# Two graph-attention layers over 64 graphs: a round laid out anew by engine, the caps on ScalarE, another column order for the left sides, and another start

## The chip, the cores and the metric

The kernel runs on one core of a Trainium2 chip. The time is the device time of one launch in microseconds, the median of three runs. A core has five engines with a queue each: TensorE (PE) multiplies matrices, VectorE (DVE), ScalarE (ACT) and GpSimd (POOL) work on elements, and SyncE (SP) here only issues transfers. Each engine takes its queue strictly in order, and engines wait for each other through semaphores.

## The reference

There are 64 graphs of N = 256 nodes with D = 512 features, and an adjacency matrix `adj` of zeros and ones for each. Two residual layers follow each other:

```python
h = jnp.maximum(_layernorm(x, axis=-1), 0.0)
x = x + _L0_gnn_ref(adj, h, ...)     # two GAT layers
h = jnp.maximum(_layernorm(x, axis=-1), 0.0)
x = x + _L1_gnn_ref(h, adj, ...)     # one attention layer, 8 heads of 64
```

The first GAT layer has 4 heads of 256 features (512 -> 1024, then elu), the second one head (1024 -> 512). For each head `e = leaky_relu(asrc[s] + adst[d])`, where `asrc` and `adst` are products of the projected features with the attention vectors. It is masked by `adj` with the diagonal set, and a softmax over the sources s is applied to the projected features. The last layer does the same with 8 heads, but its mask is `adj` alone, its softmax runs over the other axis, and a row without neighbours gets equal weights. Everything is float32.

## The kernel before

`short_path` does the work; `general_path` is entered only when an exponential leaves a safe range, which these inputs don't cause.

Graphs are handled one at a time on 128 partitions, as T = 2 tiles of 128 nodes. A graph goes through four products and three attentions:

- `m1a` and `m1b`: the normalised input times the two halves of W1 (heads 0 and 1, heads 2 and 3), then `gat1`;
- `m2`: the elu output times W2, then `gat2`;
- `m3`: the normalised sum times W_proj, then `gat3`.

**A product** (class `Product`) is a 2x2 block product with seven block multiplications in place of eight. The left side `a` holds seven blocks: four are turned parts of h, the other three and one replaced block are sums, made by `left` on GpSimd (L208 to L215). The right side `w` holds seven as well, made once by `right` on DVE (L489). The seven multiplications are the steps p1 to p7. p1, p6, p7 and p4 add into one PSUM tile `sum`; between them ACT copies the sum out (`kept`, L60: s1, u2, u3). p2, p5 and p3 go to tiles `pm`. `put` adds a copy and a `pm` on DVE (L246), or copies the sum on ACT (L244), into `xl`. In the code's order p3 may start only when c22 has read the same `pm`, p7 only when u2 is copied, and p6 and p5 only when GpSimd has made s2 and s1.

The columns that give `asrc` and `adst` ride along as extra columns of W (four in m1a, one in m2, eight in m3). They are computed at the start as dot products on DVE (`dot`, L494; for W_proj on GpSimd and DVE, L555 and L557).

**An attention** takes the logits, makes three exponentials on ACT (L268, L430) and sends one of them through DRAM to all partitions (`spread`, L233 and L238: a transfer out, and one or more transfers back into `bc`). exp(leaky_relu(a+o)) is then a maximum of two products: for each head and source tile ACT scales the row (`wy`, L273), and DVE takes the maximum and applies the mask (L274). That makes `e`. TensorE multiplies `e` by `xl` (`gat1` L348, `gat2` L399, `gat3` L447), where a column of ones gives the sum of the softmax. `gat3` works with tiles 64 columns wide, the others with 128. DVE divides (`out1` L356 and L358, `out2` L405 and L408, `out3` L453 and L455), and for `out3` GpSimd adds the result to x2 (L457). `elu1` follows on ACT and DVE (L361, L362, L367).

**masks** (L289 to L299) makes, from the integer matrix, `mask` with the diagonal and `a01` without it, counts each row (`deg`), and scales `a01` to the caps of layer three: a huge number where there is an edge, and a tiny one in every column of a row without neighbours. `cap3` turns the caps with transposing DMAs.

**The turns.** h of layer one (`norm1`, L186) is turned by a trip through DRAM (`away`, L200 and L201) that changes the order of blocks, and a 32x32 block transpose on DVE (`back`, L206). The z tiles of `turn2` and h of `turn3` are turned by TensorE (L193) and copied by ACT (L376, L226).

**What sets the order.** The kernel schedules by hand: each engine's queue is the order in which the Python code issues. `order` is a list of items, such as `-2 edges3 0`, and is gone through once for each round r; the number is added to r to give the graph. A round therefore mixes layer three of graph r-2, layer two of r-1 and the first of r. The pieces of the weight work (`weights_for_0`, `weights_for_1`) are issued one after each item in rounds 0 and 1, the rest ahead of turn2 and turn3.

**Buffers.** PSUM has 2 `sum`, 4 `pm` and 2 `pt` tiles. `e` has eight buffers, `wy` three, and the copies s1, u2 and u3 have two each.

**The start** loads graph 0 and W1 in 32 transfers, in an order of rows that fits the block order of `away`. It makes the 32 dots for W1's extra columns, turns graph 0 by way of DRAM and begins with m1a.

Of the kernel before, what the change touches and what calls it, by code (L numbers as in the profile page):

```python
# [17 lines left out]
P = 128  # L18
# [19 lines left out]
class Product:  # L38
# [19 lines left out]
    def kept(self, name):  # L58
        s = self.work.tile([P, 268], F32, name=name)
        self.nc.scalar.activation(s[:, :self.n], self.sum[:, :self.n], AF.Copy)  # L60
        return s

    def p1(self):
        self.sum = self.ps_sum.tile([P, 512], F32, name="sum")
        self.product(self.sum, 0, True, False)
        self.s1 = self.kept("s1")
# [10 lines left out]
    def p6(self):  # L77
        self.product(self.sum, 2, False, False)
        self.u2 = self.kept("u2")

    def p7(self):
        self.product(self.sum, 4, False, False)
        self.u3 = self.kept("u3")
# [14 lines left out]
def short_path(ctx, tc, flags, x, adj, w1, att_src1, att_dst1, b1, w2, att_src2, att_dst2, b2, w_proj, w_att,  # L98
# [84 lines left out]
    def norm(src, rstd, off):  # L183
        h = work.tile([P, T, D], F32, name="h", bufs=1)
        for t in range(T):
            nc.scalar.activation(h[:, t, :], src[:, t, :], AF.Relu, bias=off[:, t:t + 1],  # L186
                                 scale=rstd[:, t:t + 1])
        return h
# [6 lines left out]
    def away(h):  # L195

        kept = dram.tile([T, 4, P, P], F32, name="kept_h")
        nc.sync.dma_start(kept.rearrange("t a p e -> p t a e"), h.rearrange("p t (a e) -> p t a e", a=4))  # L200
        nc.sync.dma_start(h, kept.rearrange("t a (j q) e -> (a j) t (q e)", q=4))  # L201
# [74 lines left out]
    class Graph:  # L276


        def __init__(self, b):
            self.b = b  # L280

# [6 lines left out]
        def masks(self):  # L288

            self.mask = work.tile([P, T, N], BF16, name="mask")  # L290
            nc.vector.scalar_tensor_tensor(self.mask, self.ad, 0.0, eye, ALU.is_gt, ALU.max)
            a01 = self.a01 = work.tile([P, T, N], BF16, name="a01", bufs=1)
            nc.vector.tensor_scalar(a01, self.ad, 0.0, None, ALU.is_gt)
            deg = small.tile([P, T], F32, name="deg")
            nc.vector.tensor_reduce(deg, a01, AX.X, ALU.add)
            none = small.tile([P, T], F32, name="none")
            nc.vector.tensor_scalar(none, deg, 0.5, EVEN, ALU.is_lt, ALU.mult)
            for t in range(T):
                nc.vector.tensor_scalar(a01[:, t, :], a01[:, t, :], OPEN, none[:, t:t + 1], ALU.mult, ALU.add)  # L299
# [12 lines left out]
        def norm1(self):  # L312
            self.h = norm(self.xs, *self.ro)
# [7 lines left out]
        def turn1(self):  # L321
            a = left_of(self.h, True)
            self.m1 = [Product(nc, ps_sum, ps_mm, work, a, w1_sb[i], put1(i)) for i in range(2)]
            self.e = {}
# [12 lines left out]
        def edges1(self, h):  # L337
            e = self.e[1, h] = work.tile([P, T, N], F32, name="e", bufs=8)
            for s in range(T):
                weigh(e[:, s, :], self.bc1[h], self.ex1[:, h, s:s + 1], self.ex1[:, H1 + h, s:s + 1],  # L340
                      self.mask[:, s, :], ALU.mult)

        def gat1(self, g, t):
            self.pms = []
            for h in (2 * g, 2 * g + 1):
                pm = ps_mm.tile([P, 512], F32, name="pm")
                for s in range(T):
                    nc.tensor.matmul(pm[:, :Q + 1], self.e[1, h][:, s, t * P:(t + 1) * P], xl1[:, s, h, L1:],  # L348
                                     start=(s == 0), stop=(s == T - 1))
                self.pms.append((h, pm))  # L350

        def out1(self, g, t):
            z = self.zt[t]
            for h, pm in self.pms:
                r = small.tile([P, 1], F32, name="r1")
                nc.vector.reciprocal(r, pm[:, Q:Q + 1])  # L356
                sl = slice(h * F1, (h + 1) * F1)
                nc.vector.scalar_tensor_tensor(z[:, sl], pm[:, :Q], r, b1_sb[:, sl], ALU.mult, ALU.add)  # L358

            ez = work.tile([P, 2 * F1], F32, name="ez")  # L360
            nc.scalar.activation(ez, z[:, 2 * g * F1:2 * (g + 1) * F1], AF.Relu, scale=-1.0)  # L361
            nc.scalar.activation(ez, ez, AF.Exp, scale=-1.0)  # L362
            self.e["ez", g, t] = ez
# [21 lines left out]
        def edges2(self):  # L385
            e = self.e[2] = work.tile([P, T, N], F32, name="e", bufs=8)
            for s in range(T):
                weigh(e[:, s, :], self.bc2[0], self.ex2[:, 0, s:s + 1], self.ex2[:, 1, s:s + 1],
                      self.mask[:, s, :], ALU.mult)

        def gat2(self, t):
            if t == 0:
                self.x2 = work.tile([P, T, D], F32, name="x2")
            self.pms = []
            for half in range(2):
# [5 lines left out]
                self.pms.append(pm)  # L401

        def out2(self, t):
            r = small.tile([P, 1], F32, name="r2")
            nc.vector.reciprocal(r, self.pms[0][:, Q:Q + 1])  # L405
            for half in range(2):
                sl = slice(half * Q, (half + 1) * Q)
                nc.vector.scalar_tensor_tensor(self.x2[:, t, sl], self.pms[half][:, :Q], r, self.xs[:, t, sl],  # L408
# [10 lines left out]
        def norm3(self):  # L419
            self.h = norm(self.x2, *self.ro)  # L420
# [13 lines left out]
        def edges3(self, h):  # L434
            e = self.e[3, h] = work.tile([P, T, N], F32, name="e", bufs=8)
# [4 lines left out]
        def gat3(self, a, t):  # L440
            pm = self.pm = ps_mm.tile([P, 512], F32, name="pm")
# [8 lines left out]
        def out3(self, a, t):  # L450
            pv = self.pm[:, :G * (K3 + 1)].rearrange("p (h k) -> p h k", h=G)
# [21 lines left out]
    def bring(w, src, at, r, by, squares=False):  # L473

        nk, n = w.shape[2], w.shape[3]
        for half in range(2):
            dst = blocks(w)[r][half][:, :, n - Q:]
            cols = src[:, at + half * Q:at + (half + 1) * Q]
            if squares:
                for a in range(4):  # L480
                    by[half].dma_start(dst[32 * a:32 * (a + 1)], cols[a * P:(a + 1) * P].rearrange(
                        "(c i) f -> i c f", c=4)[:, r * nk:(r + 1) * nk])
            else:
                by[half].dma_start(dst, cols.rearrange("(c p) f -> p c f", p=P)[:, r * nk:(r + 1) * nk])
# [12 lines left out]
    att2 = [work.tile([P, D2], F32, name="e", bufs=8) for i in range(2)]  # L497
# [3 lines left out]
    for r in range(2):  # L501
        for i in range(2):
            bring(w1_sb[i], w1, 2 * Q * i, r, (nc.sync, nc.scalar), squares=True)
        if r == 0:
            nc.scalar.dma_start(att1[1].rearrange("p h f -> p (h f)"), rows_of(att_dst1, HF))
    graphs[0].stats1()
    graphs[0].norm1()
    graphs[0].away1()
# [9 lines left out]
    for r in range(2):  # L518
        for s in range(2):
            for h in range(H1):  # L520
                for c in range(2):
                    dot(blocks(w1_sb[0])[r][s][:, c, h:h + 1], blocks(w1_sb[h // 2])[r][h % 2][:, c, -Q:], att1[s][:, h, :])
            if r == 1 and s == 0:
                graphs[0].turn1()
# [3 lines left out]
    def weights_for_0():  # L528
        yield from right(w1_sb[1])
        graphs[0].masks()  # L530
        graphs[0].bias()
# [14 lines left out]
    def weights_for_1():  # L546
# [17 lines left out]
        -1 exp2, -2 edges3 0, 0 m1a p2, 0 m1a p5, -2 edges3 1, 0 m1a p6, -2 edges3 2, 0 m1b p1,  # L564
        -2 edges3 3, 0 m1a p7, 0 m1a c22, -2 edges3 4, 0 m1b p2, 0 m1a p4, 0 m1a p3, 0 exp1, -2 edges3 5,
        -2 gat3 0 0, -2 out3 0 0, 0 m1b p6, -1 edges2, -2 edges3 6, 0 m1b p5, -2 gat3 0 1, -2 out3 0 1, -2 edges3 7,
        0 m1b p7, 0 m1b c22, -1 gat2 0, -1 out2 0, -1 stats3 0, 0 edges1 0, 0 m1b p4, 0 m1b p3,
        -1 gat2 1, 0 edges1 1, -1 out2 1, 0 edges1 2, 0 edges1 3, 1 load, 0 gat1 0 0, 0 out1 0 0, -2 gat3 1 0,
        -2 out3 1 0, 0 cap3, -1 stats3 1, 0 gat1 0 1, -1 norm3, 0 out1 0 1, -2 gat3 1 1, 0 elu1 0 0, -2 out3 1 1, -2 store,
        0 gat1 1 0, 0 out1 1 0, -1 turn3, 0 elu1 0 1, 0 gat1 1 1, 0 out1 1 1, 0 elu1 1 0, 0 elu1 1 1,  # L570
        -1 m3 p1, 1 stats1, -1 m3 p2, 0 turn2 0 0, 0 turn2 0 1, -1 m3 p5, -1 m3 p6, 0 turn2 1 0, 0 turn2 1 1,
        1 norm1, 1 away1, 0 m2 p1, -1 m3 p7, -1 m3 c22, 1 masks, 0 m2 p2, -1 m3 p4, -1 m3 p3, -1 exp3,
        -2 range, 0 m2 p6, 0 m2 p5, 1 turn1, 0 m2 p7, 0 m2 c22, 1 m1a p1, 0 m2 p4, 1 bias, 0 m2 p3
    """
    graphs[0].m1[0].p1()
    order = [item.split() for item in order.split(",")]
    later = {0: (weights_for_0(), "turn2"), 1: (weights_for_1(), "turn3")}
    for r in range(B + 2):
        pieces, by = later.get(r, (iter(()), ""))
        for off, what, *args in order:  # L580
            b = r + int(off)
            if not 0 <= b < B:
                continue
            if what == by:
                for _ in pieces:
                    pass
# [8 lines left out]
            next(pieces, None)  # L595
# [274 lines left out]
```

## Time and profile before

| | before |
|---|---|
| time, median of 3 | 3387.74 us (3386.66 to 3388.05) |
| span of the profiled execution | 3383.4 us |
| PE busy | 3230.2 us (95%) |
| DVE busy | 2503.5 us (74%) |
| ACT busy | 1868.1 us (55%) |
| POOL busy | 1245.1 us (37%) |
| the masks op L291, mean of 64 | 1620 ns |
| norm1 and norm3, L186, mean | 811 and 807 ns |

In the profile's lines the first number of a timeline row is its start, the second its length, both in us, and the brackets give idle time of the engine and what ended it. A float32 multiplication appears as two instructions. Matmuls are pipelined: the length of one row overlaps the next, so the distance between two starts is what an item really costs. A row of a stretch gives the busy time of the engines in the order PE, PEld (weight loads, which overlap PE), DVE, ACT, POOL, then the granted clock of TensorE, the share of the DMA engines and GB/s.

### The profile page before, as it was taken

How to read it: one execution, taken by the hardware profiler on the slowest of the kernel's cores; microseconds unless marked ns; L12 is line 12 of the kernel's file. 1: busy time of each engine (PE TensorE's matmuls, PEld its weight loads, DVE VectorE, ACT ScalarE, POOL GpSimd, SP SyncE). 2: the span in 40 equal slices, each digit the busy share in tenths (PEclk: the TensorE clock that was granted, in tenths of full speed). 3: DMA queues.
4: the chain of work that ended last, by engine and by line, in shares of the span. 5: the costliest groups of instructions: out<-in, count | busy, mean ns of one | idle time of the engine just before them, and what ended most of it. 6: DMA issues, size and time to landing. Idle time of an engine off the chain costs nothing. (4 is left out here: it accounts for less than half of the span.)

```text
span 3383.4 us, 60097 instructions
## 1 busy us (share of the span) xinstructions
PE 3230.2 (95%) x21764; PEld 2659.8 (79%) x21764; DVE 2503.5 (74%) x6447; ACT 1868.1 (55%) x4481; POOL 1245.1 (37%) x1369
## 2 busy tenths in 40 slices
PE   4899999999999999999999999999999999999996
PEld 3688888888878888878888888888888888888885
DVE  7577777777777777787777777777777777777774
ACT  2355555555565565565565565565555555555553
POOL 1433433433433433433433434434334334334332
PEclk8999999999999999999999999999999999999997
DMA  4223333323323323323333233232333333332331
GB/s 131 63 86 83 83 81 88 82 81 82 89 76 83 91 78 83 89 80 83 85 84 84 82 87 83 81 88 78 86 88 78 87 83 83 87 82 84 86 73 47
DMA packets 354349, 281.41 MB, mean 83 GB/s; under 512 B 159616, under 2 KB 254848, under 8 KB 354048
## 3 DMA queue, kind: packets, MB, share of 16 engines
q1 hardware_dynamic: 352480, 275.40, 30.1%
q8 instruction: 177, 2.90, 0.4%
q10 hardware_dynamic: 1568, 2.10, 0.2%
q14 instruction: 124, 1.02, 0.1%
HBM read 201.07 MB, written 67.96 MB: 80 GB/s over the span
## 5 line engine op out<-in xcount | busy, mean ns | idle before, releaser
L273 ACT ACTIVATE wy<-bc,exs 128x256 f32<-128x256 f32 x1664 | 776.5, 521 | 257.5 <-DMA bc<-kept 142.1
L457 POOL TENSOR_TENSOR x<-x,o 128x256 f32<-128x256 f32 x256 | 198.7, 776 | 1431.4 <-DVE o L455 1342.8
L274 DVE SCALAR_TENSOR_TENSOR e<-wy,exs,cap 128x256 f32<-128x256 f32 x1024 | 484.7, 511 | 140.4 <-ACT wy L273 132.8
L348 PE MATMUL pm<-xl,e 128*128 128x257 f32 x2048 | 518.8, 391 | 32.0 <-DVE r L356 24.8
L54 PE MATMUL sum<-w_sb,h1s 128*128 128x257 f32 x2048 | 493.8, 383 | 0.7 <-ACT u L60 0.7
L348 PEld LDWEIGHTS pm<-xl,e 128*128 128x128 f32 x2048 | 362.6, 190 | 118.0 <-PE pm L348 46.2
L246 DVE TENSOR_TENSOR xl<-pm,u 128x256 f32<-128x256 f32 (+2 forms) x512 | 215.3, 421 | 310.0 <-PE pm L54 249.7
L54 PEld LDWEIGHTS sum<-w_sb,h1s 128*128 128x128 f32 x2048 | 379.9, 190 | 73.7 <-issue 21.9
L54 PE MATMUL pm<-w_sb,h1s 128*128 128x257 f32 x1536 | 365.3, 379 | 0.0
L60 ACT ACTIVATE u<-sum 128x260 f32<-128x260 f32 (+3 forms) x512 | 195.4, 382 | 287.0 <-PE sum L54 281.4
L447 PEld LDWEIGHTS pm<-xl,e 128*64 128x64 f32 x8192 | 265.9, 139 | 99.1 <-issue 52.2
L54 PEld LDWEIGHTS pm<-w_sb,h1s 128*128 128x128 f32 x1536 | 291.2, 190 | 44.0
L212 POOL TENSOR_TENSOR hs<-hs 128x256 f32<-128x256 f32 x128 | 127.0, 992 | 518.0 <-DVE hs L206 330.6
L274 DVE SCALAR_TENSOR_TENSOR e<-wy,exs,mask 128x256 f32<-128x256 f32 x640 | 303.7, 524 | 17.2 <-ACT wy L273 9.9
L447 PE MATMUL pm<-xl,e 128*64 128x65 f32 x8192 | 302.1, 227 | 12.9 <-DVE e L274 12.6
L54 PE MATMUL sum<-w1a_sb,hs 128*128 128x260 f32 x1024 | 274.7, 391 | 36.1 <-DMA e<-in_L_gnn_att_src_dram 28.9
L54 PE MATMUL sum<-wp_sb,hs 128*128 128x264 f32 x1024 | 277.3, 393 | 9.3 <-ACT u L60 1.1
L54 PE MATMUL sum<-w1b_sb,hs 128*128 128x256 f32 x1024 | 277.4, 393 | 1.0 <-ACT u L60 1.0
L358 DVE SCALAR_TENSOR_TENSOR z<-pm,r,b_sb 128x256 f32<-128x256 f32 x512 | 247.8, 484 | 18.2
L54 PEld LDWEIGHTS sum<-w1a_sb,hs 128*128 128x128 f32 x1024 | 188.4, 190 | 89.4 <-ACT u L60 31.8
L367 DVE SCALAR_TENSOR_TENSOR z<-ez,z 128x512 f32<-128x512 f32 x256 | 206.7, 808 | 64.0 <-ACT ez L362 64.0
L399 PE MATMUL pm<-xl,e 128*128 128x257 f32 (+1 forms) x1024 | 244.1, 381 | 2.5 <-DVE e L274 2.5
(92 smaller groups left out, 5221.7 us busy)
## 6 DMA issues: line engine op xcount, KB each, us to landing
bc<-kept SPq DMA_DIRECT2D x384, 256.0 KB, 3.8
xs<-in_x_dram SPq DMA_DIRECT2D x64, 512.0 KB, 4.0
kept_h<-h SPq DMA_DIRECT2D x64, 512.0 KB, 3.2
h<-kept_h SPq DMA_DIRECT2D x64, 512.0 KB, 3.6
out_dram<-x SPq DMA_DIRECT2D x64, 512.0 KB, 2.8
ad<-in_adj_dram SPq DMA_DIRECT2D x64, 256.0 KB, 4.3
bc<-kept SPq DMA_DIRECT2D x64, 128.0 KB, 4.3
w_sb<-in_L_gnn_W_dram SPq DMA_DIRECT2D x4, 512.0 KB, 9.2
```

What stands on the lines that cost most here:

```text
L54: self.nc.tensor.matmul(to[:, :self.n], self.lhs[:, i, c, :], self.rhs[:, i, c, :], start=(first and c == 0), stop=(last and c == self.nk ...
L60: self.nc.scalar.activation(s[:, :self.n], self.sum[:, :self.n], AF.Copy)
L212: nc.gpsimd.tensor_tensor(s1, s3, a22, ALU.add)
L246: nc.vector.tensor_tensor(dst, pm, add, ALU.add)
L273: nc.scalar.activation(wy, bc, AF.Copy, scale=yw)
L274: nc.vector.scalar_tensor_tensor(dst, wy.rearrange("p t q -> p (t q)"), xw, mask, ALU.max, op)
L348: nc.tensor.matmul(pm[:, :Q + 1], self.e[1, h][:, s, t * P:(t + 1) * P], xl1[:, s, h, L1:], start=(s == 0), stop=(s == T - 1))
L358: nc.vector.scalar_tensor_tensor(z[:, sl], pm[:, :Q], r, b1_sb[:, sl], ALU.mult, ALU.add)
L367: nc.vector.scalar_tensor_tensor(z, self.e["ez", g, t], -1.0, z, ALU.add, ALU.max)
L399: nc.tensor.matmul(pm[:, :n], self.e[2][:, s, t * P:(t + 1) * P], xl2[:, s, half, L2:L2 + n], start=(s == 0), stop=(s == T - 1))
L447: nc.tensor.matmul(pv[q:q + 64, h, :], self.e[3, a * G + h][:, s, t * P + q:t * P + q + 64], xl3[:, s, a * G + h, :], start=(s == 0), stop ...
L457: nc.gpsimd.tensor_tensor(to, to, o.rearrange("p h k -> p (h k)"), ALU.add)
```

## The change

The change has five parts.

1. **The round's order.** The list `order` is replaced. In it the two tiles of `gat3` stand side by side, several `gat` and `out` items have other items between them, the copies and adds of m1a are spread over the end of one round and the start of the next, and `store` belongs to graph r-3. So that a `gat` may be issued before the `out` of an earlier one, `pms` becomes a dictionary by layer, group and tile. Rounds run from -1 to B+2, and the weight pieces are issued from round -1 on, one list after the other.
2. **The caps on ScalarE.** `masks` keeps two DVE ops: `a01` from the integers, and `mask` as the maximum of `a01` and the diagonal in bf16. Counting the rows, which is now a by-product of a copy on ACT, and the scaling go to ACT, and the small comparison to GpSimd, in a new item `caps` that stands between m2 c22 and exp2.
3. **Columns in another order.** Row 4p+c of W1 now goes to partition p, so that each partition reads contiguous rows, in one transfer where there were four. To fit, `norm1` reads x with a stride of four elements and writes h in the order that `away` needs.
4. **Buffers.** The copies s1, u2 and u3 share one name with four buffers; `e` has nine.
5. **The start.** Graph 0 is normalised by `norm0` and turned by TensorE (`turn0`) without the trip through DRAM. W1's second half is loaded first, and m1b of graph 0 goes first, with the dots for the extra columns issued between its steps; m1a follows in round -1.

```diff
-    def kept(self, name):
-        s = self.work.tile([P, 268], F32, name=name)
+    def kept(self):
+        s = self.work.tile([P, 264], F32, name="kept", bufs=4)
...
+    def mixed(h):
+        return h.rearrange("p (a c i) -> p a c i", a=4, c=4)
+
+    def unmixed(x):
+        return x.rearrange("p (a i c) -> p a c i", a=4, c=4)
...
-            nc.scalar.activation(h[:, t, :], src[:, t, :], AF.Relu, bias=off[:, t:t + 1],
-                                 scale=rstd[:, t:t + 1])
+            to, of = (mixed(h[:, t]), unmixed(src[:, t])) if mix else (h[:, t, :], src[:, t, :])
+            nc.scalar.activation(to, of, AF.Relu, bias=off[:, t:t + 1], scale=rstd[:, t:t + 1])
...
-            self.mask = work.tile([P, T, N], BF16, name="mask")
-            nc.vector.scalar_tensor_tensor(self.mask, self.ad, 0.0, eye, ALU.is_gt, ALU.max)
             a01 = self.a01 = work.tile([P, T, N], BF16, name="a01", bufs=1)
             nc.vector.tensor_scalar(a01, self.ad, 0.0, None, ALU.is_gt)
+            self.mask = work.tile([P, T, N], BF16, name="mask")
+            nc.vector.tensor_tensor(self.mask, a01, eye, ALU.max)
+
+        def caps(self):
+            a01 = self.a01
             deg = small.tile([P, T], F32, name="deg")
-            nc.vector.tensor_reduce(deg, a01, AX.X, ALU.add)
+            for t in range(T):
+                same = work.tile([P, N], BF16, name="same", bufs=1)
+                nc.scalar.activation(same, a01[:, t, :], AF.Copy, accum_out=deg[:, t:t + 1])
             none = small.tile([P, T], F32, name="none")
-            nc.vector.tensor_scalar(none, deg, 0.5, EVEN, ALU.is_lt, ALU.mult)
+            nc.gpsimd.tensor_scalar(none, deg, 0.5, EVEN, ALU.is_lt, ALU.mult)
             for t in range(T):
-                nc.vector.tensor_scalar(a01[:, t, :], a01[:, t, :], OPEN, none[:, t:t + 1], ALU.mult, ALU.add)
+                nc.scalar.activation(a01[:, t, :], a01[:, t, :], AF.Identity, bias=none[:, t:t + 1], scale=OPEN)
...
+        def turn0(self):
+            a = work.tile([P, 7, DC // 2, P], F32, name="hs")
+            for t in range(T):
+                pm = ps_mm.tile([P, 512], F32, name="pm")
+                for c in range(DC):
+                    nc.tensor.transpose(pm[:, c * P:(c + 1) * P], self.h[:, t, c * P:(c + 1) * P], ident)
+                nc.scalar.activation(a[:, 4 * t:4 * t + 2].rearrange("p r k m -> p (r k m)"), pm, AF.Copy)
+            left(a, DC // 2)
+            self.products1(a)
...
-            if squares:
-                for a in range(4):
-                    by[half].dma_start(dst[32 * a:32 * (a + 1)], cols[a * P:(a + 1) * P].rearrange(
-                        "(c i) f -> i c f", c=4)[:, r * nk:(r + 1) * nk])
-            else:
-                by[half].dma_start(dst, cols.rearrange("(c p) f -> p c f", p=P)[:, r * nk:(r + 1) * nk])
+            rows = src[:, at + half * Q:at + (half + 1) * Q].rearrange("(p c) f -> p c f" if mix else "(c p) f -> p c f", p=P)
+            by[half].dma_start(blocks(w)[r][half][:, :, n - Q:], rows[:, r * nk:(r + 1) * nk])
...
+    m1b = graphs[0].m1[1]
+    for part in (m1b.p1, m1b.p2, m1b.p5, m1b.p6, m1b.p7, m1b.c22, m1b.p4, m1b.p3):
+        part()
+        for d in dots[:4]:
+            column(*d)
+        del dots[:4]
...
-        -1 exp2, -2 edges3 0, 0 m1a p2, 0 m1a p5, -2 edges3 1, 0 m1a p6, -2 edges3 2, 0 m1b p1,
-        -2 edges3 3, 0 m1a p7, 0 m1a c22, -2 edges3 4, 0 m1b p2, 0 m1a p4, 0 m1a p3, 0 exp1, -2 edges3 5,
-        -2 gat3 0 0, -2 out3 0 0, 0 m1b p6, -1 edges2, -2 edges3 6, 0 m1b p5, -2 gat3 0 1, -2 out3 0 1, -2 edges3 7,
-        0 m1b p7, 0 m1b c22, -1 gat2 0, -1 out2 0, -1 stats3 0, 0 edges1 0, 0 m1b p4, 0 m1b p3,
-        -1 gat2 1, 0 edges1 1, -1 out2 1, 0 edges1 2, 0 edges1 3, 1 load, 0 gat1 0 0, 0 out1 0 0, -2 gat3 1 0,
-        -2 out3 1 0, 0 cap3, -1 stats3 1, 0 gat1 0 1, -1 norm3, 0 out1 0 1, -2 gat3 1 1, 0 elu1 0 0, -2 out3 1 1, -2 store,
-        0 gat1 1 0, 0 out1 1 0, -1 turn3, 0 elu1 0 1, 0 gat1 1 1, 0 out1 1 1, 0 elu1 1 0, 0 elu1 1 1,
-        -1 m3 p1, 1 stats1, -1 m3 p2, 0 turn2 0 0, 0 turn2 0 1, -1 m3 p5, -1 m3 p6, 0 turn2 1 0, 0 turn2 1 1,
-        1 norm1, 1 away1, 0 m2 p1, -1 m3 p7, -1 m3 c22, 1 masks, 0 m2 p2, -1 m3 p4, -1 m3 p3, -1 exp3,
-        -2 range, 0 m2 p6, 0 m2 p5, 1 turn1, 0 m2 p7, 0 m2 c22, 1 m1a p1, 0 m2 p4, 1 bias, 0 m2 p3
+        0 m1a c22, -3 store, -2 edges3 2, 0 m1a p2, -2 edges3 4, 0 m1a p3, -2 edges3 3, 0 m1a p4, 0 exp1, -2
+        edges3 6, 0 m1b p2, -2 edges3 5, 0 m1b p6, -2 gat3 0 1, -2 gat3 0 0, 0 m1b p5, -2 out3 0 1, -1
+        edges2, -2 edges3 7, -2 out3 0 0, 0 m1b p7, -1 gat2 0, 0 m1b c22, -1 out2 0, -1 stats3 0, 0 m1b p3,
+        0 cap3, 0 edges1 0, -1 gat2 1, 0 edges1 1, -1 out2 1, 0 edges1 3, 0 m1b p4, 0 gat1 0 0, 0 edges1 2,
+        1 load, -2 gat3 1 0, 0 out1 0 0, -2 gat3 1 1, 0 gat1 0 1, -1 stats3 1, -1 norm3, -2 out3 1 0, -2
+        range, 0 out1 0 1, 0 gat1 1 0, -1 turn3, 0 elu1 0 0, -2 out3 1 1, 0 gat1 1 1, 0 out1 1 0, 0 elu1 0
+        1, -1 m3 p1, 0 out1 1 1, 1 stats1, -1 m3 p2, 0 elu1 1 1, 0 elu1 1 0, 1 masks, -1 m3 p6, 0 turn2 0 0,
+        0 turn2 0 1, -1 m3 p5, 1 norm1, 0 m2 p1, 0 turn2 1 0, 1 away1, 0 turn2 1 1, -1 m3 p7, -1 m3 c22, 0
+        m2 p2, -1 m3 p4, -1 m3 p3, -1 exp3, 0 m2 p6, 0 m2 p5, 1 bias, 1 turn1, 0 m2 p7, 1 m1a p1, 0 m2 p4, 0
+        m2 c22, 1 caps, 0 m2 p3, 0 exp2, 1 m1a p6, -1 edges3 0, -1 edges3 1, 1 m1b p1, 1 m1a p7, 1 m1a p5
-    graphs[0].m1[0].p1()
+    done = {"load", "stats1", "norm1", "away1", "turn1", "m1b"}
+    pieces = {"turn2": weights_for_0(), "turn3": weights_for_1()}
+    for r in range(-1, B + 3):
...
```

## The prediction

> **What bounds the kernel now.** I read first the shares of busy time, then the table of stretches in the middle of the run, then TensorE's own timeline through one round, then the sums of waits.
>
> ```profile
> PE 3230.2 (95%) x21764; PEld 2659.8 (79%) x21764; DVE 2503.5 (74%) x6447; ACT 1868.1 (55%) x4481; POOL 1245.1 (37%) x1369
> ...
> PEclk8999999999999999999999999999999999999997
> ```
>
> TensorE is the bound and runs at full clock except at both ends. The stretches of 51 us show that every round is alike:
>
> ```profile
> 1000.00:1051.00 51.00, 50.05 (x342) 41.33 (x341) 38.48 (x99) 29.19 (x70) 19.29 (x21) 1.00 0.31 83
> 2000.00:2051.00 51.00, 50.05 (x342) 41.36 (x341) 38.37 (x99) 29.16 (x71) 19.27 (x21) 1.00 0.31 84
> ```
>
> DVE has 38.4 us of work in 51, ACT 29.2, POOL 19.3. The first column of the timeline is the start, so the distance between starts, not the busy time, is what an item costs:
>
> ```profile
> 1661.32 1.13 PE L348 MATMUL pm<-xl,e 128*128 128x257 f32 x4
> 1662.80 1.10 PE L348 MATMUL pm<-xl,e 128*128 128x257 f32 x4 [0.35 <-DVE r L356]
> 1663.84 1.15 PE L447 MATMUL pm<-xl,e 128*64 128x65 f32 x32
> 1664.92 2.00 PE L348 MATMUL pm<-xl,e 128*128 128x257 f32 x8
> 1666.78 0.33 PE L193 MATMUL pt<-ident,h 128*128 128x128 f32 x1
> 1667.48 0.98 PE L193 MATMUL pt<-ident,h 128*128 128x128 f32 x7 [0.38 <-ACT h L186]
> 1668.30 1.90 PE L348 MATMUL pm<-xl,e 128*128 128x257 f32 x8
> 1670.33 1.16 PE L54 MATMUL sum<-wp_sb,hs 128*128 128x264 f32 x4
> ```
>
> The same item comes back 50.99 us later (1660.23 and 1711.22 for one L447). Unhindered, a group of four matmul instructions takes 0.89 us of m1a and m3, 0.87 of m1b and 0.87 for half of an eight of 1.74 (m2, L348, L399); eight transposes take 0.87; 32 of L447 take 1.08; and each of the four visits to L447 costs its neighbours 0.2 more (0.97 for a four before and after it). All of a round at these prices is 48.8 us. The other 2.2 us are idle: 0.5 ahead of the second L348 above (a PSUM buffer that DVE had to empty), 0.6 at the first transpose (norm3 not done), 0.3 ahead of m3 p1 (copy of the turned h), 0.26 ahead of m1b p2, and 0.5 in pieces of about 0.1. Sixty-three rounds times 50.99 are 3212 of the 3383 us.
>
> The start and end: TensorE's first matmul is at 28.89, and there is one long hole later:
>
> ```profile
> 28.89 2.10 PE L54 MATMUL sum<-w1a_sb,hs 128*128 128x260 f32 x4 [28.89 <-DMA e<-in_L_gnn_att_src_dram]
> ...
> 113.40 2.07 PE L54 MATMUL pm<-w1a_sb,hs 128*128 128x260 f32 x4 [11.47 <-DVE xl L246]
> ```
>
> The last instruction of graph 0's m2 ends at 95.7; that of graph 63 at 3323.2; so the first rounds hold 3227.5 - 3212.4 = 15 us beyond 63 steady rounds.
>
> **What the Trainium skill says.** "ScalarE: Activation LUTs", What ACT_TABLE_LOAD costs: an activation takes 186 ns + 0.833 ns per element, 93 ns more for each per-partition operand, and back-to-back ones overlap by 93. The trace agrees: L186 (two operands, 512) has a mean of 807 to 811 against 799 by that rule; L244 (none, 256) 372 against 399. "SBUF — State Buffer", Who interferes with whom: an op with two SBUF inputs, or in a two-port mode, on VectorE shuts out GpSimd and is shut out. The trace agrees: L291 takes 685 ns at its fastest, while GpSimd idles, and 1651 in the median, beside GpSimd's sums of h1s. Same page, Door 1: lines of 16 bytes, beyond which a stride is paid for. Not shown here for ScalarE: L273 reads with a stride of 8 bytes at 521 ns against 492 by the rule above; the new norm1 reads with 16. "TensorEngine Tiling (Array Packing)", Key Properties: changing the tiling mode drains TensorE; the 0.2 us around each L447 agrees.
>
> **The change, part by part.**
>
> *Two mode changes less.* The new order puts gat3 0 1 and gat3 0 0 side by side, and gat3 1 0 and 1 1. Two visits in place of four: 4 x 0.2 becomes 2 x 0.2, so a round without stalls is 48.8 - 0.4 = 48.4.
>
> *The stalls of the new order.* I walk it with t = 0 at the start of m2 p4. A result can be read 0.2 us after its last matmul's slot (m2 p3's slot ends at 1691.69, DVE starts at 1691.89). Pitches: edges 0.40 DVE and 0.43 ACT each; DVE add 0.34; out1 1.2; out2 1.05; out3 0.55; bn_stats with aggregate 0.85; ACT copy of a sum 0.31 to 0.39.
> - TensorE: m2 p3 ends at 3.5, m1a p6 4.4, m1b p1 5.2, then m1a p7.
> - *caps* stands ahead of exp2 on ACT. Not in the trace. Lower bound: two copies at 0.31, a round trip to POOL (0.2 for so small an op, L180's 195 ns, plus two hand-overs of 0.1), two scalings at 0.40: from 2.3 to 4.1, when exp2's own input is ready (m2 p3's add, 4.1): no cost. Upper bound: each copy also pays 0.2 to put its sum away, and POOL's sums are in its way 0.3: exp2 at 5.0. I take 4.7. Then exp2 0.3 and u2's copy 0.39, done at 5.4, so m1a p7 waits 0.2 (0 to 0.5). edges3, queued behind on ACT, are late by as much.
> - m1a p3 waits for c22, which needs u3, queued on ACT behind edges3 0 and 1 (4 x 0.43) and another copy: 0.1.
> - From here ACT (18 edges, 5 copies, exp1: 9.7 us to t = 15.1), then DVE are full. edges3 3 ends at 11.4, gat3 wants it at 11.9. edges2 ends at 15.0, gat2 at 15.9. exp1 ends at 11.2; its two DMAs took 7.2 us before (exp1 1700.11 to the first wy at 1707.28): 18.4. edges1 1 ends at 21.1; gat1 0 0 takes its second head at 21.9. stats3 1 ends at 26.0, rstd and off 1.0, norm3 1.5: 28.55. turn3 is due at 28.64, so the 0.6 us stall of before goes, with 0.1 to spare.
> - The copies of turn3 end on ACT at 30.9, POOL's s1 and s2 (1.26 and 0.73 in the trace) at 32.9; m3 p6 is due at 33.0. gat1's PSUM buffers come free by 28.0 to 29.2, before use: the 0.5 us stall goes.
> - The later products have 0.5 to 0.9 us to spare: m2 p6 needs POOL's s2 at 42.2 and is due at 42.7; m1a p1 needs the turned h at 47.1 and is due at 47.9.
> Named stalls: 0.2 + 0.1 + 0.1 = 0.4. To these I add the small pieces of 0.1 that before has too, 0.5: 48.4 + 0.9 = **49.3 us** a round.
>
> *masks.* L291 (1651) and L295 to L299 (686 + 182 + 2 x 300) leave DVE; a TENSOR_TENSOR on bf16 comes in, between 0.35 and 0.69. DVE falls by some 2.5 us a round, ACT rises by 1.6 to 2. Neither is the bound at that place (between elu1 and m3 c22 DVE waits for TensorE: L246 waits 250 us for it), so this is worth nothing by itself; its price is the wait at exp2.
>
> *norm1's order.* Same instruction count, read in steps of 16 bytes. Lower bound: no cost. Upper bound: half speed, + 0.43 us each, 0.9 us a round: m2 p6 and m1a p1 then use up their 0.5 and 0.8. I take none, as stride 8 cost 29 ns in L273.
>
> *kept with four buffers, nine e, pms by key:* four copies are alive at most (m1a's three and m1b's s1), seven plus two e; nothing waits. Cost zero, hidden by gat1 and gat3 freeing e before edges1 ask.
>
> *The start.* W1 comes by 8 transfers in place of 32, and graph 0 skips the trip through DRAM (20.96 to 27.7). norm0 can run at 9.9 in place of 19.4, m1b begins at about 16 in place of m1a at 28.9. But m1a waits for all 32 dots (0.35 each, 0.9 while transfers crowd) and the sums on w1a (2.9), and DVE stands in order behind m1b's adds: I get m1a p3's add at 42, exp1 at 43 against 48.9, a gain of 6. The products of w_att (16 x 0.7 on DVE, and 9 us until att3 is there) move from round 1, where they are the hole at 113.40, into round 0, where they lie in graph 0's own chain: some 3 us gained. Sum 9 (2 to 20). The end is the same chain of edges and DMA: 0.
>
> **The sum.** 63 x (50.99 - 49.3) = 106, plus 9, plus 0: 3387.7 - 115 = about 3272.
>
> **The rivals.**
> - *Floor.* Everything is hidden and the small pieces go too: 48.4 a round, and 15 at the start: 3388 - 163 - 15 = 3210. For it: all margins in the walk are positive. Against it: they are 0.1 us at two places.
> - *ScalarE takes the place.* norm1 pays for its stride and caps reach their upper bound: + 0.6 at m2 p6 and + 0.4 at m1a p7, a round of 50.3: 3388 - 43 - 9 = 3336. For it: caps sit in front of exp2, the start of the longest chain of edges. Against it: the 8-byte stride is nearly free.
> - *The chain from exp2 to turn3 becomes the bound, slower than before.* From 5.4 to 28.6 DVE has 18.7 us of work; before, the same chain took 22.6 from the first edge to stats3 1 (1693.2 to 1715.8, 3.3 of it idle), and I allow 20.1. If the new interleaving leaves it 23.5 (it waits for ACT as in the 142.8 us of L274 behind L273), turn3 is 3.4 late: 48.4 + 0.9 + 3.4 = 52.7 - and some of that falls on stalls already counted: 51.7. 3388 + 45 - 9 = 3424. Against it: ACT is given edges in an order that never leaves it behind DVE by more than three buffers.
>
> **How the numbers follow.** Forecast 0.62, floor 0.12, ScalarE 0.17, slower chain 0.08, no change 0.01 (it would need the losses to meet the gains by chance). The range reaches from near the floor, 3218, to the ScalarE case, 3335. Faster 0.91, same 0.01, slower 0.08.
>
> **What would show it.** Rounds of 49 to 49.6 in the stretches, with TensorE busy for nearly all; the waits of transposes for norm3 and of L348 for DVE gone or under 0.2; two visits of 64 instructions of gat3; a wait at m1a p7 for ACT's copy of u2 of about 0.2; the mask op on DVE under 0.7 us; norm1's mean still near 0.81; exp1 of graph 0 near 43. It would be wrong if the first transposes of turn3 wait by microseconds for norm3, if norm1 is near 1.2, or if TensorE's granted clock falls in the middle of the run because it idles less.

## The result and the profile after

The changed kernel takes 3305.14 us (median, 3302.69 to 3308.74), the kernel before 3387.89 in the same comparison: ratio 0.9757, 95% interval 0.974 to 0.9774. The gain is 82.7 us; the forecast was 115, to 3272 (range 3218 to 3335).

The shares of busy time and the granted clock, from the page of the changed kernel:

```profile
PE 3153.8 (95%) x21772; PEld 2657.8 (80%) x21772; DVE 2237.4 (68%) x6189; ACT 2031.4 (61%) x4867; POOL 1172.9 (35%) x1433
...
PEclk7999999999999999999999999999999999999998
```

266 us have left DVE, ACT has 163 more, and TensorE's share stays at 95%, of a shorter span. Two stretches of 51 us; after the length come the busy times of PE, PEld, DVE, ACT and POOL, then the granted clock:

```profile
1000.00:1051.00 51.00, 49.83 (x346) 42.17 (x346) 35.23 (x97) 32.71 (x81) 18.07 (x22) 1.00 0.33 84
2000.00:2051.00 51.00, 49.44 (x344) 41.80 (x344) 34.79 (x96) 32.34 (x79) 18.08 (x22) 1.00 0.31 83
```

TensorE still idles for 1.2 to 1.6 us in each: the floor of the prediction is not reached. Where it idles, its timeline in one round shows (changed kernel):

```profile
2014.32 1.03 PE L54 MATMUL sum<-w1b_sb,hs 128*128 128x256 f32 x4
2016.17 2.00 PE L382 MATMUL pm<-xl,e 128*128 128x257 f32 x8 [0.82 <-DVE e L281]
2018.12 2.09 PE L482 MATMUL pm<-xl,e 128*64 128x65 f32 x64
2020.69 1.97 PE L382 MATMUL pm<-xl,e 128*128 128x257 f32 x8 [0.48 <-DVE r L390]
2022.91 1.98 PE L382 MATMUL pm<-xl,e 128*128 128x257 f32 x8 [0.26 <-DVE o L490]
2024.73 1.08 PE L201 MATMUL pt<-ident,h 128*128 128x128 f32 x8
```

The transposes of turn3 (L201) no longer wait for norm3, and gat3 comes as one visit of 64. But there is a wait that the kernel before hardly had: gat1 0 0 (the first L382) waits for edges1 (L281), here for 0.82 us, in other rounds for 0 to 2.1. Two more follow it, for PSUM buffers that out1 and out3 have to empty. The sums over the run, from TensorE's waits (total, times, longest):

```profile
PE pm L382 <- DVE e L281: 45.0, 56, 9.0
PE pm L382 <- DVE r L390: 34.6, 64, 2.8
PE pm L382 <- DVE o L490: 15.6, 61, 0.3
```

Together 95 us. The longest, 9.0 us, stands once, at graph 0's gat1; without it they are 1.4 us a round. The same wait for edges1 was 7.2 us in the whole run before. What edges1 wait for is one step back, in ScalarE's waits: `wy`, its first half, stood 276.7 us for `bc`, the broadcast of the exponentials, against 142.1 before. The table of transfers tells which. The last columns are the size and the median time from issue to landing. Kernel before:

```profile
out_dram<-x SPq DMA_DIRECT2D x64, 512.0 KB, 2.8
kept<-exs SPq DMA_DIRECT2D x64, 4.0 KB, 3.8
```

Changed kernel:

```profile
out_dram<-x SPq DMA_DIRECT2D x64, 512.0 KB, 8.5
kept<-exs SPq DMA_DIRECT2D x64, 4.0 KB, 6.3
```

The 4 KB are exp1's first transfer (the 1 KB and 8 KB of exp2 and exp3 did not slow down so: 3.4 to 2.9, 4.3 to 4.7). The new order puts `-3 store` on SyncE's queue just ahead of it (changed kernel, SyncE's queue):

```profile
2002.01 0.32 SPq L245 DMA_DIRECT2D bc<-kept  x1
2002.42 0.39 SPq L499 DMA_DIRECT2D out_dram<-x  x1
2005.05 0.37 SPq L240 DMA_DIRECT2D kept<-exs  x1
2011.58 0.85 SPq L245 DMA_DIRECT2D bc<-kept  x2
```

6.5 us pass from the issue of `kept` to that of `bc`. Over the 64 graphs the median of this stretch is 6.2 us, in the kernel before 3.8. (Of the landings, the changed kernel's trace gives only 7 of the 64 stores and 8 of the 64 transfers of 4 KB; the issues it gives all.)

In account: 63 rounds, measured between the first matmuls of gat2, went from 50.99 to 50.08 us in the mean (-57), and no longer all alike; graph 0's gat2 starts 14.1 us earlier (119.89 to 105.78); from graph 63's gat2 to the end it is 46.0 us in place of 50.9. Together this is 76 us, the difference of the two profiled spans (3383.4 and 3307.0).

### The profile page after: what moved, and what is told of

It reads as the page before. It is cut to its first block, busy times and chain, and to the rows that moved or that the text cites. A ratio compares the mean times of both kernels' runs of the same rounds, so it can differ in the third digit from the quotient of the medians.

```text
span 3307.0 us, 60191 instructions
## 1 busy us (share of the span) xinstructions
PE 3153.8 (95%) x21772; PEld 2657.8 (80%) x21772; DVE 2237.4 (68%) x6189; ACT 2031.4 (61%) x4867; POOL 1172.9 (35%) x1433
## 3 DMA queue, kind: packets, MB, share of 16 engines
q10 hardware_dynamic: 1376, 2.10, 0.2%
## 5 line engine op out<-in xcount | busy, mean ns | idle before, releaser
L280 ACT ACTIVATE wy<-bc,exs 128x256 f32<-128x256 f32 x1664 | 761.7, 524 | 328.6 <-DMA bc<-kept 276.7
L382 PE MATMUL pm<-xl,e 128*128 128x257 f32 x2048 | 504.9, 390 | 95.2 <-DVE e L281 45.0
L253 DVE TENSOR_TENSOR xl<-pm,kept 128x256 f32<-128x256 f32 (+2 forms) x768 | 321.1, 418 | 360.0 <-PE pm L54 285.8
L60 ACT ACTIVATE kept<-sum 128x264 f32<-128x264 f32 (+3 forms) x768 | 286.3, 381 | 399.3 <-PE sum L54 399.2
L281 DVE SCALAR_TENSOR_TENSOR e<-wy,exs,cap 128x256 f32<-128x256 f32 x1024 | 450.8, 481 | 110.2 <-ACT wy L280 110.2
L382 PEld LDWEIGHTS pm<-xl,e 128*128 128x128 f32 x2048 | 356.0, 190 | 207.8 <-DVE e L281 69.2
L281 DVE SCALAR_TENSOR_TENSOR e<-wy,exs,mask 128x256 f32<-128x256 f32 x640 | 303.2, 527 | 111.1 <-ACT wy L280 111.1
L178 POOL TENSOR_TENSOR rstd<-ve,neg_half 128x2 f32<-128x2 f32 x128 | 90.0, 703 | 670.2 <-DVE ve L176 663.8
L482 PEld LDWEIGHTS pm<-xl,e 128*64 128x64 f32 x8192 | 255.3, 139 | 57.5 <-issue 30.9
L482 PE MATMUL pm<-xl,e 128*64 128x65 f32 x8192 | 274.0, 225 | 13.2 <-DVE e L281 13.0
L54 PE MATMUL sum<-w1b_sb,hs 128*128 128x256 f32 x1024 | 264.0, 380 | 3.0 <-ACT hs L343 1.9
L395 ACT ACTIVATE ez<-z 128x512 f32<-128x512 f32 x256 | 160.1, 626 | 127.0 <-DVE z L392 127.0
```

The costliest lines, as they stand in the source:

```text
L54: self.nc.tensor.matmul(to[:, :self.n], self.lhs[:, i, c, :], self.rhs[:, i, c, :], start=(first and c == 0), stop=(last and c == self.nk ...
L178: nc.gpsimd.tensor_tensor(rstd, ve[:, 0, :], neg_half, ALU.pow)
L253: nc.vector.tensor_tensor(dst, pm, add, ALU.add)
L280: nc.scalar.activation(wy, bc, AF.Copy, scale=yw)
L281: nc.vector.scalar_tensor_tensor(dst, wy.rearrange("p t q -> p (t q)"), xw, mask, ALU.max, op)
L482: nc.tensor.matmul(pv[q:q + 64, h, :], self.e[3, a * G + h][:, s, t * P + q:t * P + q + 64], xl3[:, s, a * G + h, :], start=(s == 0), stop ...
```

## The experiments

Two theories are tested: the store delays exp1's trip through DRAM and with it edges1 (A); or the work of DVE and ScalarE from exp2 on, with caps and norm1's stride in it, makes edges1 late whatever the queue does (B). "Trip" is the median from the issue of exp1's `kept` to that of its `bc`; rounds are means of the 63. Times stand beside 3386 to 3391 us of the kernel before on the same chips, and the interval of each ratio is about 5 us to either side.

**1. The store later.**

```diff
-        0 m1a c22, -3 store, -2 edges3 2, ...
+        0 m1a c22, -2 edges3 2, ...
-        ... -2 out3 1 1, 0 gat1 1 1, ...
+        ... -2 out3 1 1, -2 store, 0 gat1 1 1, ...
```

> The store of a graph's output (512 KB) moves from between exp2's and exp1's transfers to the place after out3 1 1, where the kernel before had it. Theory A (the store, one item ahead of exp1's 4 KB on the same queue, holds up exp1's trip through DRAM, and edges1 and gat1 0 0 wait for it): issue of exp1's kept to issue of its bc falls from 6.2 to about 3.8 us, the 45 us in which gat1's matmuls wait for edges1 fall under 5, the rounds become regular at 49.1 to 49.4 in place of 50.08, time 3245 to 3265. Theory B (edges1 are late because of the work of DVE and ScalarE from exp2 on, whatever the queue does): the trip may shorten but the rounds stay at 50, time 3300 to 3310.

Measured 3198.93 us (ratio 0.9452, 0.9437 to 0.9466), 106 below the changed kernel: trip 4.1 us, most rounds 48.2, mean 48.34. The same place in TensorE's timeline, late store:

```profile
1705.71 1.03 PE L54 MATMUL sum<-w1b_sb,hs 128*128 128x256 f32 x4
1706.58 1.90 PE L382 MATMUL pm<-xl,e 128*128 128x257 f32 x8
1708.40 2.09 PE L482 MATMUL pm<-xl,e 128*64 128x65 f32 x64
1710.42 3.74 PE L382 MATMUL pm<-xl,e 128*128 128x257 f32 x16
1713.99 1.07 PE L201 MATMUL pt<-ident,h 128*128 128x128 f32 x8
```

All three waits are gone from the rounds (of the 13 us left in the run, 8.8 are one wait of graph 0's gat1), and in the two stretches TensorE is busy for 50.95 and 51.00 of 51 us. A holds, and its size was given too small: I had counted only the wait for edges1, and the two waits behind it went with it.

**2. The store moved to just behind exp1.** It passes seven items of the list.

```diff
-        0 m1a c22, -3 store, -2 edges3 2, ... 0 m1a p4, 0 exp1, ...
+        0 m1a c22, -2 edges3 2, ... 0 m1a p4, 0 exp1, -3 store, ...
```

> The smallest edit on the store: it moves over five items only, from ahead of edges3 2 to right behind exp1, so that on the queue it stands behind exp1's two transfers instead of ahead of them; nothing else moves on any engine. If it is the place ahead of exp1's transfers that costs the 106 us (exp1's trip 6.2 us, gat1 waiting), the trip is back at 3.5 to 4.1 us and the time at 3195 to 3215. If the 106 us came from the place further on (x2 set free at another time, or the store beside the load), the time stays within 3290 to 3310, or in between.

Measured 3435.88 us (1.0137, 1.012 to 1.0154), slower than the kernel before. The trip is 3.96 us and gat1 hardly waits for edges1 (9.1 us in all), as A has it, but neither time was expected. The cause is a new wait, on DVE (first line) and on TensorE behind it, in this kernel's waits:

```profile
DVE x L443 <- DMA out_dram<-x: 238.7, 61, 5.0
...
PE pm L433 <- DVE x L443: 145.6, 61, 3.5
```

`x2` has two buffers. out2 of graph b writes the buffer that the store of b - 2 reads, and the store now lands after out2 wants to start. In the changed kernel this wait is 1.7 us in the whole run: its store lands just before out2. So of these two places, ahead of exp1 and behind it, neither is free. A third buffer of `x2` was not tried. The granted clock also fell, to 0.98 in the four stretches of 500 us from 500 to 2500, where the others have 1.00. The mean round is 52.2 us, 4.0 above the 48.2 of most rounds with the late store. The second wait above and those for the buffers of out1 and out3 explain 2.7 of this; the lower clock may explain another 1.0 (an estimate, 2% of a round), but nothing here shows that apart.

**3. The store in its place, on ScalarE's queue.**

```diff
-            nc.sync.dma_start(out[self.b]...., self.x2)
+            nc.scalar.dma_start(out[self.b]...., self.x2)
```

> The store stays where the changed kernel has it, but is issued by ScalarE on its own DMA queue instead of SyncE's. If exp1's 4 KB wait for the 512 KB because both are in one queue, in order, the trip falls to 3.5 to 4.1 us and the time to 3195 to 3225 (ScalarE pays up to 0.4 us a round for the issue). If the store is in the way because it fills the DMA engines or the memory, whatever the queue, the trip stays near 6 us and the time at 3290 to 3330.

Measured 3252.1 us (0.9592, 0.9577 to 0.9607): half of the 106. Trip 4.8 us, rounds 49.20. Neither outcome came by itself, and the edit moved the store in time as well. On SyncE's queue it is issued 0.4 us behind exp2's broadcast and 2.5 us ahead of exp1's 4 KB (medians); on ScalarE's it goes 1.2 us ahead of the broadcast and 4.1 us ahead of the 4 KB. One round of this kernel, store, broadcast and 4 KB:

```profile
2016.43 0.38 ACTq L499 DMA_DIRECT2D out_dram<-x  x1
2017.79 0.32 SPq L245 DMA_DIRECT2D bc<-kept  x1
2020.49 0.37 SPq L240 DMA_DIRECT2D kept<-exs  x1
```

So the head start of 1.6 us is a rival to the separate queue as the cause of the shorter trip, and this run does not tell them apart. The stall has moved in part: exp2's broadcast now takes 5.5 us to land (4.0 in the changed kernel), and gat2, which waits for edges2 for 1.8 us in the changed kernel, does so for 10.7 us (total, times, longest):

```profile
PE pm L433 <- DVE e L281: 10.7, 12, 2.5
```

**4. A small store in its place.**

```diff
-            nc.sync.dma_start(out[self.b].rearrange("(t p) d -> p t d", p=P), self.x2)
+            nc.sync.dma_start(out[self.b].rearrange("(t p) d -> p t d", p=P)[:8], self.x2[:8])
```

> The store stays where the changed kernel has it, in SyncE's queue, but only the rows of the first 8 partitions are stored (32 KB in place of 512; the rest of the output is left out). If it is the bytes of the store that hold up exp1's 4 KB, the trip is back at 3.5 to 4.1 us and the time at 3190 to 3205. If one more item in the queue, or its issue on SyncE, is what delays, the trip stays above 5 us and the time above 3280.

Measured 3200.22 us (0.9441, 0.9427 to 0.9456), trip 4.0 us. It is the size of the store (its bytes and its packets, which nothing here separates), not one more item in the queue. With 1 and 2 this shows the cause of the 106 us: 512 KB in flight ahead of 4 KB.

**5. caps earlier, with the store in its place and with the late store.**

```diff
-        ... 0 m2 c22, 1 caps, 0 m2 p3, 0 exp2, ...
+        ... 0 m2 p5, 1 caps, 1 bias, ... 0 m2 c22, 0 m2 p3, 0 exp2, ...
```

> caps of the next graph goes from just before exp2 to the place after m2 p5, where ScalarE idles for 3.1 us. Theory A (exp1's transfers set the stall; exp1 follows from TensorE's m1a, which caps delays by under 0.1 us): exp2 starts 0.3 us earlier, and the time falls by 0 to 8 us, to 3297 to 3305. Theory B (caps ahead of exp2 starts the longest chain late): each 0.3 us is passed on to the round, 63 x 0.3 = 19 us or more, 3286 or less.

> Late store and caps after m2 p5. With the stall of exp1's trip gone TensorE runs through, so that the 0.3 us by which caps delay exp2 should be hidden: 3195 to 3204, no difference to the late store alone. If caps still delay m1a p7 by 0.1 us a round (1699.05 to 1700.00 is 0.95 against 0.87 of a group of four), 6 us come off: 3193.

Measured 3289.47 us (0.9716, 0.9702 to 0.9729), 16 less than the changed kernel, and 3189.72 (0.9412, 0.9399 to 0.9425), 9 less than the late store alone. With the store in its place the gain lies between the two theories' figures: caps ahead of exp2 cost some 0.25 us a round (the mean round falls by 0.29). With the late store the time is below both figures given. Most rounds go from 48.20 to 48.12, the 0.08 by which m1a p7 waited; the rest of the 9 is fewer irregular rounds (mean 48.34 to 48.20). So B has a small part, 9 to 16 us beside A's 106. The second of these is the fastest kernel of the study.

**6. norm1 without its stride**, in the changed kernel, with the late store, and in the old order (experiment 8).

```diff
-            self.h = norm(self.xs, *self.ro, True)
+            self.h = norm(self.xs, *self.ro, False)
```

> norm1 reads and writes whole rows with no stride, as norm3 does, so from graph 1 on the columns meet the wrong rows of W1 (values differ, the work is the same); all else as in the changed kernel. norm1 falls from 1.33 to 0.81 us an instruction. Theory A (the stride is hidden, since TensorE hardly waits for the turned h: 1.2 us in the whole run): 3300 to 3306. Theory B (it is passed on through POOL's h1s and the turned h): 1 us a round at most, down to 3245.

> Late store, and norm1 without its stride (whole rows read and written as norm3 does; from graph 1 on the columns meet the wrong rows of W1, the work is the same). With exp1's stall gone TensorE runs through, so the 0.5 us that each norm1 instruction saves on ScalarE should show nowhere: 3193 to 3203, as the late store alone (3199). If a wait for the turned h had been hidden behind the stall of before, up to 0.5 us a round, 30 us, come off.

The stride is not free on ScalarE; norm1's instructions (count, then busy us and mean ns), first in the changed kernel:

```profile
L195 ACT ACTIVATE h<-xs,off,rstd 128x512 f32<-128x512 f32 x126 | 161.3, 1331 | 4.0 <-POOL off L180 1.3
```

Then the late store without the stride:

```profile
L195 ACT ACTIVATE h<-xs,off,rstd 128x512 f32<-128x512 f32 x126 | 95.7, 807 | 4.0 <-POOL off L180 1.3
```

But 3306.47 us (0.9769, 0.9755 to 0.9782) and 3201.72 (0.9444, 0.9431 to 0.9457) are no different from 3305 and 3199: in the new order the microsecond a round is hidden, both times.

**7. gat3 pulled apart, with the late store.**

```diff
-        ... -2 gat3 0 1, -2 gat3 0 0, 0 m1b p5, ... -2 gat3 1 1, 0 gat1 0 1, ...
+        ... -2 gat3 0 1, 0 m1b p5, -2 gat3 0 0, ... 0 gat1 0 1, -2 gat3 1 1, ...
```

> On top of the late store (3199, where TensorE hardly waits): the two gat3 of each pair are pulled apart again, one item between them, so that TensorE goes into 64-column tiles four times a round and not two. If each visit costs its drain, 0.2 us, the round goes from 48.2 to 48.6 and the time up by 63 x 0.4 = 25 us, to 3224. If the drain is hidden by weight loads, no change: 3195 to 3204.

Measured 3232.01 us (0.9538, 0.9523 to 0.9552), 33 more; rounds almost all at 48.85, with TensorE hardly waiting. Two visits more cost 0.65 us in most rounds, 0.33 each: the cost of a visit is real, and dearer than the 0.2 that I had read from its neighbours. The rest lay inside the visit: two visits of 32 took 1.08 us each (1663.84 to 1664.92 in the prediction's lines), one of 64 takes 2.02 (1708.40 to 1710.42 in experiment 1), 0.14 less than the two.

**8. The old order, with and without norm1's stride.**

```diff
     order = """
-        (the order of the changed kernel)
+        (the order of the kernel before, with 1 caps after 1 masks)
```

> Everything of the change but the order: the items are in the order of the kernel before, with caps right after masks. It splits the gain into order and the rest. If the order is what shortens the rounds, they are back at 51 to 51.5 (norm1's stride and caps may add to ScalarE's chain), and only the start remains, -10 to -19: 3368 to 3395. If the work taken from DVE shortens the rounds by itself, they fall under 50.5 and the time under 3350.

> The old order with all other parts of the change (3417), and norm1 without its stride (columns against the wrong rows of W1 from graph 1 on). There TensorE waited 38 us for the turned h and 28 us for norm3. If norm1's stride is what the old order could not hide, the first wait falls under 10 us and the time by 30 to 45 us, to 3372 to 3390; if it is caps behind masks on ScalarE, the time stays above 3405.

Measured 3417.36 us (1.0089, 1.0074 to 1.0105) and 3360.53 (0.9918, 0.9903 to 0.9933). The first time is outside both figures that I gave. Without the order the change loses, and what loses is norm1's stride: 57 us, more than the 30 to 45 that I expected. In the old order TensorE waits for the turned h (total, times, longest; the kernel with the stride):

```profile
PE sum L54 <- DVE hs L213: 38.4, 33, 3.0
```

Without the stride this wait, two thirds of the 57 us, is gone, and the rounds are regular again, at 50.76. What is left of the change's other parts in the old order is a mean round of 50.77 in place of 50.99, 14 us, and a start 10.1 us earlier (first gat2 at 109.78).

**9. The kernel before, with its store ahead of exp1 and one round later.**

```diff
-        ... 0 m1a p3, 0 exp1, ... -2 out3 1 1, -2 store, ...
+        ... 0 m1a p3, -3 store, 0 exp1, ... -2 out3 1 1, ...
...
-    for r in range(B + 2):
+    for r in range(B + 3):
```

> The kernel before, with one edit: its store goes ahead of exp1, one round later, the place that the changed kernel gives it. If a bulk store ahead of exp1's trip delays edges1 in any order, the trip goes from 3.8 to about 6 us and the time up by 20 to 130 us, to 3410 to 3520, or more if out2 has to wait for x2 as well. If the old order has slack enough there, it stays within 3380 to 3395.

Measured 3425.56 us (1.0111, 1.0095 to 1.0126), 35 more. The trip goes from 3.8 to 4.9 us, less than the 6 expected, and the store's landing from 2.8 to 7.9. The edit costs in the old order too. TensorE's wait for edges1 (L274) goes from 7.2 to 24.3 us, about half of the 35; the other half was not traced.

## Why the prediction was right in size and wrong on the way

The ledger that the runs give, in steps: masks, caps, buffers and the start, in the old order and without the stride, 3388 to 3361 (-27); the stride, +57; the new order with the store left late, -218, to 3199; the store at its new place, +106, to 3305. Of the 218, 57 are the stride again, which the new order hides: without the stride the same step is 3361 to 3202.

That the forecast of 3272 was near is luck. A stall of 106 us was put at 0, and 73 us that the new order gains beyond the forecast (3272 to 3199) were not counted; the two errors ran against each other. The rounds alone brought 57 us where the sum had 106.

- **The step that failed: exp1's trip.** "exp1 ends at 11.2; its two DMAs took 7.2 us before [...]: 18.4. edges1 1 ends at 21.1; gat1 0 0 takes its second head at 21.9." The duration was carried over from the old order, but `-3 store` now stands ahead of exp1 in the list, and I walked the engines item by item without walking SyncE's queue. From exp1's start to the first `wy` it is now 10.3 us in the round shown (2004.82 to 2015.08 on ScalarE), and 7.9 with the late store. A margin of 0.8 can't take the 3.1 more than the 7.2 assumed. Cost: 106 us, which I had at 0.
- **Mode changes.** Right in kind, 0.2 each in the sum, measured 0.33; the part inside the visit was hidden in the price of 1.08.
- **The stalls of the new order, 0.9 a round.** They are not there. With the store out of the way the round is 48.2; the floor of 48.4 was 48.8 less two visits at 0.2, and at the measured 0.33 it is 48.15. Of the named stalls, m1a p7's wait for u2 was 0.08 in place of 0.2; the 0.5 of small pieces had been carried over from the old order and went with it. (The 0.26 us of before, given as ahead of m1b p2, lie ahead of m1a p4, at 1697.18; the sum is the same.)
- **norm3 and the PSUM buffer.** turn3's wait went from 28.3 us to 4.0, as walked. The PSUM wait did not go (34.6 us for out1's reciprocal, 24.8 before) until the store was moved (2.9).
- **masks.** "Worth nothing by itself" is nearly so: in the old order all the parts that touch the rounds bring 14 us together. Its TENSOR_TENSOR took 426 ns, inside the 350 to 690 given, but only in the new order: in the old one it takes 1346 (last section). DVE fell by about 4 us a round, not 2.5; of the rest, 1.0 is L299, which dropped from 1455 ns (old L293) to 415, by its new place as well.
- **caps.** Each copy pays for its sum as the upper bound had it: 413 ns, and 190 more for an instruction of its own that reads the accumulator. exp2 starts 0.3 us after its input, inside the bounds (the terms of the upper bound add up to 4.8, not to the 5.0 given); the price is 9 to 16 us.
- **norm1.** "I take none, as stride 8 cost 29 ns in L273" is wrong by 520 ns an instruction, beyond the upper bound of 430 that I had given. It costs nothing in this order and 57 us in the old one. The walk had margins of 0.5 and 0.8 for it, and 1.0 us a round fits in without cost, so they must have been larger than I had them.
- **The start and end.** exp1 of graph 0 is at 44.1 (43 in the walk), m1b begins at 15.4 (16), the hole at 113.40 is gone. The first gat2 gained 14.1 and the end 4.9, together 19 where 9 + 0 was in the sum. The end was not expected to move; with the change's other parts in the old order it hardly does (51.6 and 50.3 us from the last gat2), so it belongs to the order.

The rival in which ScalarE takes the place gave 3336, and the measured time lies between it and the forecast, but not for its reason: the stride costs nothing here and caps 9 to 16 us.

Of the three signs that I had listed for a failure, two stayed out: in the rounds the first transposes of turn3 don't wait by microseconds for norm3, and the granted clock stays at 1.00 through the middle of the run. The other one came: norm1 is at 1.33 us, past the 1.2 named, and it cost nothing in this order, so it was no sign of failure. Of the signs of success, rounds of 49 to 49.6 and the end of gat1's wait for DVE stayed out (50.08; 0.48 us for out1's reciprocal in the round shown). The sign that would have caught the failure, gat1 waiting for edges1, was not on the list.

## What to carry to other kernels

Where results go through DRAM and back on a transfer queue, that round trip is a step of the schedule like any instruction: walk the queue too, and look at what bulk transfer a new order puts ahead of a small one. Moving the bulk transfer has its own end, the buffer that it reads: look for who writes that buffer next. And a cost that an order hides (the stride: 0 here, 57 us there) should be priced in the order in which it will run; so should an operation whose time hangs on what another engine does beside it (the mask: 426 ns here, 1346 there).

## What the runs showed of the hardware

- A 512 KB store ahead of a 4 KB write lengthened the time to the write's landing from 3.8 to 6.3 us (medians), and its own from 2.8 to 8.5 (8 and 7 landings known in the changed kernel; the trip, known for all 64, goes from 3.8 to 6.2). From another queue, and issued 1.6 us earlier, the store took 4.6 and the 4 KB 4.5, but exp2's broadcast 5.5 in place of 4.0. With a store of 32 KB the trip was short again (4.0 us). How much lies in the queue, in the DMA engines and in the memory stays open.
- ScalarE reading 512 float32 in steps of 16 bytes: 1331 ns against 807 to 811 without. The Trainium skill, "SBUF — State Buffer", Door 1, has lines of 16 bytes beyond which a stride is paid for, and gives 4 float32 as how far one can stride for free; the prediction leaned on that. For this read on ScalarE the measurement decides, and 16 bytes already pay. The same passage asks for at least two hits in a line, and that agrees with both numbers: a stride of 8 bytes hits each line twice (521 ns, prediction), one of 16 once. So stride 8 was no guide to stride 16. The strided read is also cut into 16 runs of 32 elements, which no run tells apart from the stride.
- The two mask operations on DVE took 415 (L299, the int32 compare) and 426 ns (L301) in the changed kernel, where GpSimd idles beside all 64 of each. In experiment 8, with the same instructions in the old order, L301 takes 1376 ns in the median beside GpSimd's sums of h1s, and 425 in the two of 64 times when GpSimd idles. First the changed kernel, then experiment 8 with the stride:

```profile
L301 DVE TENSOR_TENSOR mask<-a,eye 128x512 bf16<-128x512 bf16 x64 | 27.2, 426 | 2.2
L301 DVE TENSOR_TENSOR mask<-a,eye 128x512 bf16<-128x512 bf16 x64 | 86.1, 1346 | 2.2
```

The compare took 1455 in the mean in the kernel before, 1490 in the median beside GpSimd's sums and 419 in the one case without. "Who interferes with whom" on the same page agrees. So a price of such an operation holds only for what GpSimd does at its place in the round. No run took GpSimd's work away alone.
- In experiment 2, where TensorE waited 2.7 us a round and up to 3.5 at once, its granted clock was 0.98 through the middle of the run; in the changed kernel, with 1.4 us of waits a round, and in the old order with the change's other parts (waits up to 3.0) it stayed at 1.00. What sets it is open.
